# A graph layer and masked attention on one core: the row maximum is taken off the mask once, instead of off every score

## The chip, the core and the metric

The kernel runs on one core of a Trainium2 chip. Every time is in device microseconds (us) for one execution of the whole program; single instructions are given in nanoseconds (ns) where that reads better. A core has five engines with a queue each, worked off in order: TensorE (PE in the profile; PEld is its weight load) multiplies matrices into PSUM, VectorE (DVE) and ScalarE (ACT) read and write both PSUM and SBUF, GpSimd (POOL) works on SBUF only, and SyncE (SP) issues most of the DMAs. PSUM has eight banks of 128 partitions x 512 fp32 numbers. An engine waits for another through semaphores.

## What is computed

Two layers over 64 batch elements of 256 tokens with 512 features, all in fp32. The first mixes tokens with an adjacency matrix, the second is attention with 8 heads of 64 under a mask that is made of the same matrix. Cut to what matters here:

```python
h = jnp.maximum(_layernorm(x, axis=-1), 0.0)
x = x + einsum('bnd,do->bno', einsum('nm,bmd->bnd', adj, h), W0) + b0      # layer 0
h = jnp.maximum(_layernorm(x, axis=-1), 0.0)                               # layer 1
q = (h @ Wq + bq).reshape(b, n, H, HD)          # k and v in the same way
scores = einsum('bqhd,bkhd->bhqk', q, k) / sqrt(HD)
scores = scores + (1.0 - adj)[None, None, :, :] * -1000000000.0
attn = softmax(scores, axis=-1)
x = x + einsum('bhqk,bkhd->bqhd', attn, v).reshape(b, n, d) @ Wo + bo
```

The entries of `adj` are numbers between 0 and 1, not only 0 and 1. So the mask (1 - adj) * -1e9 differs by far more than any score between two entries of a row, and nearly all of a row's weight falls on its largest mask entry. A softmax may subtract any number from a row. The kernel doesn't subtract the maximum of the scores but the maximum of the mask's row, which it finds once.

## The kernel before

The 64 batch elements are taken in 32 groups of two (`NG = 32`, `GB = 2`). Layer 0 runs over all groups first (the loop `for g in range(NG - 1)`), then layer 1 over all groups.

**Order by hand.** The program text is the order of every engine's queue. The work that follows a matrix product (moments, exponentials, sums) is put later with `after(delay, ...)`, which queues a call for a later `tick()`. Pieces of work that belong to no group go into `side[g]`: the mask is prepared in seven steps at `side[20]` to `side[26]`, each issued on VectorE at the start of the turn of one group of layer 0. The products of layer 1 follow orders written out as strings (`QK` for queries and keys, `VO`, `V1`, `O1`, `OL` for values and outputs). A token such as `qGe` is one instruction: q is the product, G a block of it, e a step. `x` in these strings issues the next waiting exponential on ScalarE (`next_exponent`). 30 of the 32 groups get their queries and keys by `QK`, which holds this stretch:

```python
"... kGa x qCe qGc kCe qGd kCf kGi qCf kGj | qGe kGk kGb qFk kCg qp100 qGf kCh ..."
```

`qGe` is a copy of half the bank `q_Gs` by ScalarE (line 690), and `qGf` a matrix product (line 653) that adds into that half. It has to wait for the copy.

**Banks.** `bank()` hands out the PSUM banks in the order in which they were given back. With `seed=` it takes only a bank that was written as a whole last time, and ScalarE writes the seed into it (line 306); the first matmul then adds to what is there (`start=False`). `give()` puts a bank back when its last reader has been issued.

**Scores.** `score(g, qd)` is called 64 times (32 groups, `qd` for half of the heads). It makes four score blocks (c, b), each of two banks, with keys on the partitions and queries along the row. For blocks (0,0) and (0,1) ScalarE first fills four banks with the mask divided by the scale (`score_seeds`), TensorE adds the scores (line 1176), and VectorE's eviction multiplies by the scale and subtracts the row maximum `top` (line 1184). Blocks (1,0) and (1,1) get no seed: VectorE's eviction multiplies and adds the mask `maskT` (line 1187), and a further instruction subtracts `top` from the block of 128 x 1024: on GpSimd (line 1194) in 125 cases, on VectorE (line 1192) in three. The exponential in place follows on ScalarE (line 1210), the sum over two key halves on GpSimd (line 1217).

**Attention.** `attend(g, qd)` multiplies the exponentials with ones (`pden`, line 1226) and with the values (`pav`, line 1233). ScalarE copies the denominator (line 1240). Logarithm, exponential and a correction step on GpSimd invert it (`invert`, lines 1248 to 1252), and VectorE multiplies (line 1271). The next `score` follows `attend` directly on TensorE.

**Check.** Sums of denominators and reciprocals are kept in `stats`. At the end one comparison with `BOUND` over all of them decides whether the whole input is computed once more by `general_path`, with an ordinary softmax. With the inputs of the reference it isn't.

Of the kernel before, what the change touches and what calls it, by code (L numbers as in the profile page):

```python
# [8 lines left out]
F32 = mybir.dt.float32  # L9
I32 = mybir.dt.int32  # L10
AF = mybir.ActivationFunctionType
ALU = mybir.AluOpType
AX = mybir.AxisListType
P = 128
# [2 lines left out]
MASKED = -1000000000.0  # L17

BOUND = 1.0e15


def load_weight(nc, pool, w, name):
# [223 lines left out]
def kernel(  # L246
# [25 lines left out]
    HQ = 2  # L272
# [2 lines left out]

    nc.scalar.preload_act_table_set("natural_log_exp_and_others")
    keep = ctx.enter_context(tc.tile_pool(name="keep", bufs=1))
    stats = keep.tile([P, 2, NG * HQ], F32, name="stats")
    flag = keep.tile([1, 1], I32, name="flag")

    main = ExitStack()
# [14 lines left out]
    def bank(shape, name, seed=None, times=1.0, partial=False, full=False):  # L296

        if seed is not None or full:
            i = next(i for i in free_banks if whole[i])
        else:  # L300
            i = next((i for i in free_banks if not (partial and whole[i])), free_banks[0])
        free_banks.remove(i)
        t = psum.tile(shape, F32, tag=f"bank{i}", name=name)
        bank_of[id(t)] = (i, t)
        if seed is not None:
            nc.scalar.mul(t, seed, times)  # L306
        return t

    def give(t, all_written=True):
        i = bank_of.pop(id(t))[0]  # L310
        free_banks.append(i)
        whole[i] = all_written
# [5 lines left out]
    def after(delay, fn, *args):  # L318
        entered[0] += 1
        later.append((clock[0] + delay, entered[0], fn, args))  # L320
# [71 lines left out]

    maskT = const.tile([P, NT, N], F32, name="maskT")
    maskT_f = maskT.rearrange("p k n -> p (k n)")
    top = const.tile([P, N], F32, name="top")
    top_b = top[:, None, :].to_broadcast([P, 2 * NT, N])

    def masks():
        adj_sb = tmp.tile([P, NT, N], F32, tag="u", name="adj_sb")
        nc.sync.dma_start(adj_sb, adj.rearrange("(t p) m -> p t m", p=P))  # L400
        yield
        pm = bank([P, NT, N], "pm")
        for k in range(NT):
            for t in range(NT):
                nc.tensor.transpose(pm[:, k, t * P:(t + 1) * P], adj_sb[:, t, k * P:(k + 1) * P], ident)
        nc.vector.tensor_scalar(maskT, pm, -1.0, 1.0, op0=ALU.mult, op1=ALU.add)
        give(pm, False)
        yield
        nc.vector.tensor_scalar(maskT, maskT, MASKED, None, op0=ALU.mult)
        yield  # L410
        nc.vector.tensor_scalar(adj_sb, adj_sb, -1.0, 1.0, op0=ALU.mult, op1=ALU.add)
        yield
        nc.vector.tensor_scalar(adj_sb, adj_sb, MASKED, None, op0=ALU.mult)
        yield
        rowmax = small.tile([P, NT], F32, tag="rowmax", name="rowmax", bufs=1)
        nc.vector.tensor_reduce(rowmax, adj_sb, AX.X, ALU.max)
        spread = tmp.tile([P, NT, P], F32, tag="u", name="spread")
        nc.vector.tensor_copy(spread, rowmax[:, :, None].to_broadcast([P, NT, P]))
        yield
        pt = bank([P, N], "pt")  # L420
        for t in range(NT):
            nc.tensor.transpose(pt[:, t * P:(t + 1) * P], spread[:, t, :], ident)
        nc.vector.tensor_copy(top, pt)
        give(pt, False)


    L1 = {}
# [724 lines left out]

    A, AS, behind_seeds, behind_scores, exponents = {}, {}, [], [], []

    def score_bank(g, qd, c, b, **how):
        return [bank([P, NT * N], f"sc_{g}_{qd}_{c}{b}_{j}", **how) for j in range(2)]

    def score_seeds(g, qd, n=2):
        return {cb: score_bank(g, qd, *cb, seed=maskT_f, times=1.0 / SCALE) for cb in ((0, 0), (0, 1), (1, 0))[:n]}

    def score(g, qd, sums=(5, 6, 7, 8), exps=(3, 4, 5, 8), masked=None):


        pair = [act.tile([P, GB, 2 * NT, N], F32, tag="h", name=f"a_{g}_{qd}_{c}", bufs=2) for c in range(2)]

        masked = masked or score_seeds(g, qd)
        while behind_seeds:
            behind_seeds.pop(0)()
        for c in range(2):
            for b in range(GB):  # L1170
                seen = (c, b) in masked
                ps = masked[c, b] if seen else score_bank(g, qd, c, b)
                q, k = Q[g][qd, b], K[g][qd, b]
                for kt in range(NT):
                    for j in range(2):
                        nc.tensor.matmul(ps[j][:, kt * N:(kt + 1) * N],  # L1176
                                         k[j * HD:(j + 1) * HD, c, kt * P:(kt + 1) * P],
                                         q[j * HD:(j + 1) * HD, c, :], start=(kt == 0 and not seen), stop=True,
                                         skip_group_check=True)
                a = A[c, b] = pair[c][:, b]  # L1180
                for j in range(2):
                    o = a[:, j * NT:(j + 1) * NT, :]
                    if seen:
                        nc.vector.scalar_tensor_tensor(o, ps[j].rearrange("p (k n) -> p k n", k=NT), SCALE,  # L1184
                                                       top_b[:, 0:NT, :], op0=ALU.mult, op1=ALU.subtract)
                    else:
                        nc.vector.scalar_tensor_tensor(o.rearrange("p k n -> p (k n)"), ps[j], SCALE, maskT_f,  # L1187
                                                       op0=ALU.mult, op1=ALU.add)
                    give(ps[j])
                if not seen:  # L1190
                    if (g == NG - 1 or (g, qd) == (0, 0)) and b == 1:
                        after(0 if qd else 2, lambda a: nc.vector.tensor_tensor(a, a, top_b, op=ALU.subtract), a)
                    else:
                        nc.gpsimd.tensor_tensor(a, a, top_b, op=ALU.subtract)  # L1194
                if exps is None:
                    exponents.append((a, clock[0] + sums[2 * c + b], g, qd, c, b))
                else:
                    after(exps[2 * c + b], exponent, a)
                    after(sums[2 * c + b], key_sum, g, qd, c, b)
        while behind_scores:  # L1200
            behind_scores.pop(0)()
# [97 lines left out]
        side[4 + 4 * i].append((lambda n: weight_sums(nc.gpsimd, L1[n][0], n, [2 + STEPS * j for j in range(4)]), n))  # L1299
    for i in range(2):  # L1300
        side[13 + i].append((lambda: next(bias_steps, None),))
    for i in range(7):
        side[20 + i].append((lambda: next(mask_steps, None),))

    idle = bank([P, NT, N], "idle")
# [54 lines left out]
    first, second = queries_keys(0)  # L1360
    run(plain(0, *first))
    run(steps)
    second = plain(0, *second)
    run(second, 6)
    seeds = score_seeds(0, 0)
    run(second)
    score(0, 0, (4, 5, 6, 7), (3, 4, 5, 6), seeds)
    tick()
    hidden_sums(1, 6, 6, 7, 7)
    run(plain(0, *values(0)))  # L1370
# [1 line left out]
    for g in range(NG):  # L1372
# [2 lines left out]
        if g + 2 < NG:  # L1375
            load_hidden(g + 2)
        if g == NG - 1:
            score(g, 1, (2, 3, 5, 4), (1, 2, 4, 3), score_seeds(g, 1, 2))
        else:
            score(g, 1, exps=None if g + 1 >= FIRST2 else (3, 4, 5, 8))  # L1380
        tick()
# [26 lines left out]
            run(last)  # L1408
        attend(g, 1)
        if g + 1 < NG:  # L1410
            score(g + 1, 0, (5, 6, 7, 8) if g + 1 < NG - 1 else (1, 1, 1, 1), None if g + 1 >= FIRST2 else (3, 4, 5, 8),
                  score_seeds(g + 1, 0, 2) if g + 1 == NG - 1 else None)
            tick()

            def multiplied(g=g):
                del HH[g + 1]
                H2.pop(g + 1, None)
                if g + 2 < NG:
                    hidden_sums(g + 2, 1, 1, 1, 1)
                    if g + 2 >= FIRST2:  # L1420
                        block_hidden(g + 2, 2)

            n, halves, *rest = values(g + 1)
            if g + 1 < FIRST2:
                steps = plain(g + 1, n, halves, *rest)
                run(steps, 5)
                seeds = seed_outputs(g)
                run(steps)
                multiplied()
            else:  # L1430
                steps = quartered(g + 1, n, halves, H2[g + 1], *rest, multiplied=multiplied)
                if FIRST2 <= g < NG - 2:
                    steps.update(quartered_outputs(g))
                    run(follow(steps, VO))
                else:
                    steps = follow(steps, V1)
                    run(steps, 6)
                    if g < FIRST2:
                        seeds = seed_outputs(g)
                    run(steps)  # L1440
            if g < FIRST2:
                run(plain_outputs(g, seeds))
# [1 line left out]
    last = follow(quartered_outputs(NG - 1), OL)  # L1444
    run(last, 2)

    bad = small.tile([P, 2 * NG * HQ], F32, tag="bad", name="bad", bufs=1)
    worst = small.tile([P, 1], F32, tag="worst", name="worst", bufs=1)
    nc.vector.tensor_scalar(bad, stats.rearrange("p s i -> p (s i)"), BOUND, None, op0=ALU.is_le)
    nc.vector.tensor_reduce(worst, bad, AX.X, ALU.min)  # L1450
    nc.vector.tensor_scalar(worst, worst, -1.0, 1.0, op0=ALU.mult, op1=ALU.add)
    run(last, 3)
# [39 lines left out]
```

## Time and profile before

| what | value |
|---|---|
| median of three runs | 2607.23 us (2605.9 to 2607.35) |
| the profiled execution, device time | 2605.43 us |
| its span from first to last instruction | 2603.7 us |
| start of the first score (layer 1 under way) | 637.5 us |
| ScalarE seeds of score banks, line 306 | 256 x 591 ns |
| VectorE evictions, line 1184 with `top` / line 1187 with `maskT` | 256 x 684 ns / 256 x 681 ns |
| GpSimd subtractions of `top`, line 1194 | 125 x 2368 ns |
| VectorE subtractions of `top`, line 1192 | 3, of 1.22 to 2.30 us |
| exponentials waiting for line 1194 | 12.2 us in 37 waits, longest 0.7 |

A share of busy time says what an engine did, not what it held up: GpSimd is 80% busy, and most of this may lie beside TensorE's work. What counts for the time is where TensorE starts later than it could. Such a place can hide in a busy share, since the records of successive matmuls overlap: it shows as a longer mean of one group, or as a longer step from one start to the next.

### The profile page before, as it was taken

What the parts mean: (1) busy time and instruction counts of PE and PEld (TensorE: products, weight loads), DVE (VectorE), ACT (ScalarE), POOL (GpSimd) and SP (SyncE); (2) the same over time, 40 slices, a digit from 0 to 9 for tenths busy, and PEclk for the clock granted to TensorE, in tenths of its full rate; (3) what the DMA queues carried; (4) which work ended last, traced back from release to release, by engine and by line L of the source; (5) the groups of instructions that cost most, each with busy time, mean ns of one, the idle gap of its engine ahead of it and who ended that gap; (6) DMA issues with size and microseconds to landing.
All of it is one profiled execution on the core that took longest, in us unless ns stands there. A gap on an engine that the chain in (4) does not pass through costs nothing.

```text
span 2603.7 us, 57470 instructions
## 1 busy us (share of the span) xinstructions
PE 2586.1 (99%) x21914; PEld 2303.6 (88%) x21914; DVE 1908.9 (73%) x4154; ACT 1381.1 (53%) x3198; POOL 2082.9 (80%) x2275
## 2 busy tenths in 40 slices
PE   8999999999999999999999999999999999999998
PEld 7999899998888888888888888888888888888886
DVE  6888888885566777777776777777776777777777
ACT  4545454443455555555555555555555555555553
POOL 6788887774798888888877888888888888888776
PEclk9999999999999999999999999999999999999999
DMA  5776666565112222111111111111122222111101
GB/s 147 194 195 183 167 170 181 161 163 126 33 51 60 62 60 64 50 50 50 50 50 50 50 50 50 50 50 50 49 52 66 62 61 58 50 50 50 50 34 50
DMA packets 281112, 211.40 MB, mean 81 GB/s; under 512 B 145920, under 2 KB 212992, under 8 KB 280832
## 3 DMA queue, kind: packets, MB, share of 16 engines
q1 hardware_dynamic: 280224, 206.89, 30.0%
q8 instruction: 175, 2.87, 0.5%
q10 hardware_dynamic: 608, 0.79, 0.1%
q14 instruction: 105, 0.86, 0.1%
HBM read 106.96 MB, written 100.66 MB: 80 GB/s over the span
## 4 chain that ended last, share of the span: by engine, by line


## 5 line engine op out<-in xcount | busy, mean ns | idle before, releaser
L1184 DVE SCALAR_TENSOR_TENSOR a<-sc,top 128x512 f32<-128x512 f32 x256 | 159.0, 684 | 261.8 <-PE sc L1176 257.8
L1217 POOL TENSOR_TENSOR as<-a 128x512 f32<-128x512 f32 x256 | 319.5, 1280 | 6.3 <-ACT a L1210 6.2
L1194 POOL TENSOR_TENSOR a<-a,top 128x1024 f32<-128x1024 f32 x125 | 293.3, 2368 | 36.3 <-DVE a L1187 36.3
L1250 POOL TENSOR_TENSOR as<-as 128x512 f32<-128x512 f32 x64 | 80.5, 1258 | 267.3 <-ACT as L1249 263.8
L1210 ACT ACTIVATE a<-a 128x1024 f32<-128x1024 f32 x256 | 272.0, 1063 | 18.1 <-POOL a L1194 12.2
L1176 PE MATMUL sc<-q,k 64*128 64x256 f32 x2048 | 239.4, 383 | 0.0
L1176 PEld LDWEIGHTS sc<-q,k 64*128 64x128 f32 x2048 | 196.5, 187 | 43.5 <-issue 26.3
L1233 PE MATMUL pav<-a,v 128*32 128x256 f32 x4096 | 232.7, 379 | 0.0
L1233 PEld LDWEIGHTS pav<-a,v 128*32 128x32 f32 x4096 | 133.1, 110 | 87.9
L1240 ACT ACTIVATE as<-pden 128x512 f32<-128x512 f32 x64 | 38.4, 599 | 286.4 <-PE pden L1226 286.4
L42 DVE BATCH_NORM_STATS2 st<-x 128x6 f32<-128x512 f32 x256 | 173.2, 676 | 9.0 <-DMA x<-in_x_dram 6.8
L1187 DVE SCALAR_TENSOR_TENSOR a<-sc,maskT 128x512 f32<-128x512 f32 x256 | 158.4, 681 | 0.0
L1007 ACT ACTIVATE h<-x,nb,rs 128x512 f32<-128x512 f32 x128 | 97.2, 807 | 98.6 <-POOL nb L54 98.5
L306 ACT ACTIVATE sc<-maskT 128x512 f32<-128x512 f32 x256 | 137.4, 591 | 0.0
L878 ACT ACTIVATE h<-x,nb,rs 128x512 f32<-128x512 f32 x124 | 90.8, 803 | 52.1 <-POOL nb L54 46.6
L941 POOL TENSOR_TENSOR hs<-h 128x512 f32<-128x512 f32 x31 | 39.4, 1270 | 73.0 <-ACT h L878 73.0
L1013 DVE STREAM_TRANSPOSE r<-h 128x512 f32<-128x512 f32 x128 | 84.5, 691 | 8.9 <-ACT h L1007 3.6
L1097 ACT ACTIVATE q<-q_pa,bq_c 128x256 f32<-128x256 f32 (+1 forms) x150 | 61.8, 456 | 49.2 <-PE q_pa L653 36.9
L1271 DVE TENSOR_TENSOR oT<-pav,as 128x512 f32<-128x512 f32 x128 | 82.2, 683 | 7.7 <-POOL as L1252 7.5
L602 POOL TENSOR_TENSOR spare<-h1T,spare 128x128 f32<-128x128 f32 x180 | 82.1, 456 | 7.0
L826 DVE TENSOR_TENSOR x<-o_pa,x 128x512 f32<-128x512 f32 (+1 forms) x121 | 82.5, 682 | 6.0 <-PE o_pa L667 4.9
L503 POOL TENSOR_TENSOR t_y<-yT,t_y 128x512 f32<-128x512 f32 (+1 forms) x65 | 83.0, 1276 | 2.8 <-ACT yT L913 0.3
(1630 smaller groups left out, 8735.1 us busy)
## 6 DMA issues: line engine op xcount, KB each, us to landing
residual<-x SPq DMA_DIRECT2D x256, 128.0 KB, 2.7
hidden<-r SPq DMA_DIRECT2D x128, 256.0 KB, 4.5
h1T<-hidden SPq DMA_DIRECT2D x64, 512.0 KB, 7.5
x<-residual SPq DMA_DIRECT2D x32, 1024.0 KB, 8.1
x<-in_x_dram SPq DMA_DIRECT2D x254, 128.0 KB, 3.0
out_dram<-x SPq DMA_DIRECT2D x62, 512.0 KB, 4.1
w_sb<-in_L_gnn_weight_dram SPq DMA_DIRECT2D x1, 1024.0 KB, 9.9
wq_sb<-in_L_gnn_Wq_dram SPq DMA_DIRECT2D x1, 1024.0 KB, 8.4
```

The costliest lines, as they stand in the source:

```text
L42: nc.vector.bn_stats(st, src)
L306: nc.scalar.mul(t, seed, times)
L878: nc.scalar.activation(H0[g][:, t, :], xt[:, t, :], AF.Relu, bias=nb[:, t % n:t % n + 1], scale=rs[:, t % n:t % n + 1])
L1007: nc.scalar.activation(h1[:, k * NT + t, :], xt[:, k * NT + t, :], AF.Relu, bias=nb[:, t:t + 1], scale=rs[:, t:t + 1])
L1013: nc.vector.transpose(r[:, :, k, t, :], h1[:, k * NT + t, :].rearrange("p (j b) -> p j b", b=32))
L1176: nc.tensor.matmul(ps[j][:, kt * N:(kt + 1) * N], k[j * HD:(j + 1) * HD, c, kt * P:(kt + 1) * P], q[j * HD:(j + 1) * HD, c, :], start=(kt ...
L1184: nc.vector.scalar_tensor_tensor(o, ps[j].rearrange("p (k n) -> p k n", k=NT), SCALE, top_b[:, 0:NT, :], op0=ALU.mult, op1=ALU.subtract)
L1187: nc.vector.scalar_tensor_tensor(o.rearrange("p k n -> p (k n)"), ps[j], SCALE, maskT_f, op0=ALU.mult, op1=ALU.add)
L1194: nc.gpsimd.tensor_tensor(a, a, top_b, op=ALU.subtract)
L1210: nc.scalar.activation(a, a, AF.Exp)
L1217: nc.gpsimd.tensor_tensor(AS[c, b], a4[:, :, 0, :], a4[:, :, 1, :], op=ALU.add)
L1233: nc.tensor.matmul(po[f][h * 32:(h + 1) * 32, b * N:(b + 1) * N], v[:, k, h * HD + f * 32:h * HD + f * 32 + 32], A[h // 2, b][:, (h % 2) * ...
```

## The change

The row maximum is subtracted from the mask itself, once, when the mask is prepared: `maskT` then holds mask minus row maximum. All four score blocks are now evicted in the same way: scale, add `maskT`. The seeds on ScalarE, the tile `top` and the separate subtractions on GpSimd and VectorE are gone. With that a score block takes any two banks that are free, two at a time, and its first matmul overwrites.

The sums are not the same in rounding: before, the score was added to a mask entry of up to 1e9 in size, and lost its small digits, before the maximum was taken off. So two new steps of the preparation (now nine, at `side[20]` to `side[28]`) count in each row the mask entries within 1000 (`CLOSE`) of the maximum. A row with more than one, unless its maximum is 0, sets an entry of `ties` to 1e20. `ties` lies behind `stats` in one tile, `checks`, and the comparison with `BOUND` at the end covers both.

```diff
-    top = const.tile([P, N], F32, name="top")
-    top_b = top[:, None, :].to_broadcast([P, 2 * NT, N])
...
     def masks():
...
-        nc.vector.tensor_copy(top, pt)
+        for k in range(NT):
+            nc.vector.tensor_tensor(maskT[:, k, :], maskT[:, k, :], pt, op=ALU.subtract)
         give(pt, False)
+        yield
+        near = small.tile([P, NT], F32, tag="near", name="near", bufs=1)
+        nc.vector.tensor_scalar(near, rowmax, -CLOSE, None, op0=ALU.add)
+        for t in range(NT):
+            nc.vector.tensor_scalar(adj_sb[:, t, :], adj_sb[:, t, :], near[:, t:t + 1], None, op0=ALU.is_ge)
+        yield
+        nc.vector.tensor_reduce(near, adj_sb, AX.X, ALU.add)
+        nc.vector.tensor_scalar(near, near, -1.0, None, op0=ALU.add)
+        nc.vector.tensor_tensor(near, near, rowmax, op=ALU.mult)
+        nc.vector.tensor_tensor(near, near, near, op=ALU.mult)
+        nc.vector.tensor_scalar(ties, near, 1.0, 1.0e20, op0=ALU.min, op1=ALU.mult)
...
-    def score_bank(g, qd, c, b, **how):
-        return [bank([P, NT * N], f"sc_{g}_{qd}_{c}{b}_{j}", **how) for j in range(2)]
-
-    def score_seeds(g, qd, n=2):
-        return {cb: score_bank(g, qd, *cb, seed=maskT_f, times=1.0 / SCALE) for cb in ((0, 0), (0, 1), (1, 0))[:n]}
-
-    def score(g, qd, sums=(5, 6, 7, 8), exps=(3, 4, 5, 8), masked=None):
+    def score(g, qd, sums=(5, 6, 7, 8), exps=(3, 4, 5, 8)):
...
-                seen = (c, b) in masked
-                ps = masked[c, b] if seen else score_bank(g, qd, c, b)
+                ps = [bank([P, NT * N], f"sc_{g}_{qd}_{c}{b}_{j}") for j in range(2)]
...
-                                         q[j * HD:(j + 1) * HD, c, :], start=(kt == 0 and not seen), stop=True,
+                                         q[j * HD:(j + 1) * HD, c, :], start=(kt == 0), stop=True,
...
-                    if seen:
-                        nc.vector.scalar_tensor_tensor(o, ps[j].rearrange("p (k n) -> p k n", k=NT), SCALE,
-                                                       top_b[:, 0:NT, :], op0=ALU.mult, op1=ALU.subtract)
-                    else:
-                        nc.vector.scalar_tensor_tensor(o.rearrange("p k n -> p (k n)"), ps[j], SCALE, maskT_f,
-                                                       op0=ALU.mult, op1=ALU.add)
+                    nc.vector.scalar_tensor_tensor(o.rearrange("p k n -> p (k n)"), ps[j], SCALE, maskT_f,
+                                                   op0=ALU.mult, op1=ALU.add)
                     give(ps[j])
-                if not seen:
-                    if (g == NG - 1 or (g, qd) == (0, 0)) and b == 1:
-                        after(0 if qd else 2, lambda a: nc.vector.tensor_tensor(a, a, top_b, op=ALU.subtract), a)
-                    else:
-                        nc.gpsimd.tensor_tensor(a, a, top_b, op=ALU.subtract)
...
-    for i in range(7):
+    for i in range(9):
         side[20 + i].append((lambda: next(mask_steps, None),))
...
-    bad = small.tile([P, 2 * NG * HQ], F32, tag="bad", name="bad", bufs=1)
+    bad = small.tile([P, 2 * NG * HQ + NT], F32, tag="bad", name="bad", bufs=1)
...
-    nc.vector.tensor_scalar(bad, stats.rearrange("p s i -> p (s i)"), BOUND, None, op0=ALU.is_le)
+    nc.vector.tensor_scalar(bad, checks, BOUND, None, op0=ALU.is_le)
```

More of the change, by code (lines that the diff above doesn't have):

```diff
@@ L19 @@
 BOUND = 1.0e15
+CLOSE = 1000.0
 def load_weight(nc, pool, w, name):
@@ L277 @@
     keep = ctx.enter_context(tc.tile_pool(name="keep", bufs=1))
-    stats = keep.tile([P, 2, NG * HQ], F32, name="stats")
+    checks = keep.tile([P, 2 * NG * HQ + NT], F32, name="checks")
+    stats = checks[:, 0:2 * NG * HQ].rearrange("p (s i) -> p s i", s=2)
+    ties = checks[:, 2 * NG * HQ:]
     flag = keep.tile([1, 1], I32, name="flag")
@@ L1153 @@
     A, AS, behind_seeds, behind_scores, exponents = {}, {}, [], [], []
-    def score_bank(g, qd, c, b, **how):
-        return [bank([P, NT * N], f"sc_{g}_{qd}_{c}{b}_{j}", **how) for j in range(2)]
-    def score_seeds(g, qd, n=2):
-        return {cb: score_bank(g, qd, *cb, seed=maskT_f, times=1.0 / SCALE) for cb in ((0, 0), (0, 1), (1, 0))[:n]}
-    def score(g, qd, sums=(5, 6, 7, 8), exps=(3, 4, 5, 8), masked=None):
+    def score(g, qd, sums=(5, 6, 7, 8), exps=(3, 4, 5, 8)):
         pair = [act.tile([P, GB, 2 * NT, N], F32, tag="h", name=f"a_{g}_{qd}_{c}", bufs=2) for c in range(2)]
-        masked = masked or score_seeds(g, qd)
         while behind_seeds:
@@ L1362 @@
     run(steps)
[L1363 to L1367, printed above, removed]
+    run(plain(0, *second))
+    score(0, 0, (4, 5, 6, 7), (3, 4, 5, 6))
     tick()
@@ L1377 @@
         if g == NG - 1:
-            score(g, 1, (2, 3, 5, 4), (1, 2, 4, 3), score_seeds(g, 1, 2))
+            score(g, 1, (2, 3, 5, 4), (1, 2, 4, 3))
         else:
@@ L1410 @@
         if g + 1 < NG:
-            score(g + 1, 0, (5, 6, 7, 8) if g + 1 < NG - 1 else (1, 1, 1, 1), None if g + 1 >= FIRST2 else (3, 4, 5, 8),
-                  score_seeds(g + 1, 0, 2) if g + 1 == NG - 1 else None)
+            score(g + 1, 0, (5, 6, 7, 8) if g + 1 < NG - 1 else (1, 1, 1, 1), None if g + 1 >= FIRST2 else (3, 4, 5, 8))
             tick()
```

## The prediction, made before the changed kernel had run

> **What bounds the kernel now.** I read the page's shares first, then the form-by-form groups of TensorE, then stretches of the timeline where those groups differ.
>
> ```profile
> span 2603.7 us, 57470 instructions
> ...
> PE 2586.1 (99%) x21914; PEld 2303.6 (88%) x21914; DVE 1908.9 (73%) x4154; ACT 1381.1 (53%) x3198; POOL 2082.9 (80%) x2275
> ...
> PEclk9999999999999999999999999999999999999999
> ```
>
> TensorE is busy 99% of the span at full clock; only 17.6 us are idle, most of it in the first and the last 100 us. So nothing that GpSimd or ScalarE saves counts by itself: it counts where TensorE waits for it. A busy share hides short waits, because a matmul record that started late still overlaps its neighbours. The groups show them (line, engine, operation, names, shape, count, busy us, mean ns of one, idle before):
>
> ```profile
> L653 PE MATMUL q_Gs<-spare,spare 128*128 128x128 f32 x120 | 25.9, 298 | 0.0
> ...
> L653 PE MATMUL k_Gs<-spare,spare 128*128 128x128 f32 x120 | 23.2, 275 | 0.0
> ```
>
> These are the same multiplication for queries and for keys, and one is 23 ns longer on average: 120 x 23 ns = 2.8 us. The timeline of one group shows why (start, length, engine, line, what):
>
> ```profile
> 854.87 4.69 POOL L1194 TENSOR_TENSOR a<-a,top 128x1024 f32<-128x1024 f32 x2
> ...
> 859.59 1.06 ACT L1210 ACTIVATE a<-a 128x1024 f32<-128x1024 f32 x1 [0.37 <-POOL a L1194]
> ...
> 860.54 0.39 PE L653 MATMUL k_Cs<-spare,spare 128*128 128x128 f32 x2
> 860.56 0.25 ACT L690 COPY q_G<-q_Gs 128x128 f32<-128x128 f32 x1
> ...
> 860.86 0.49 PE L653 MATMUL q_Gs<-spare,spare 128*128 128x128 f32 x2
> ...
> 861.18 0.39 PE L653 MATMUL k_Gs<-spare,spare 128*128 128x128 f32 x2
> ```
>
> GpSimd's two subtractions of `top` end at 859.56. The exponential waits 0.37 us for the second, the copy of `q_Gs` stands behind the exponential on ScalarE, and TensorE may overwrite that bank only after the copy: 860.56 + 0.25 = 860.81, and it starts at 860.86. Two such matmuls normally start 0.22 us before what follows; here 0.32 pass before `q_Gs` and 0.32 within it (its pair reads 0.49 long, not 0.39): wait plus restart. From the records of single matmuls, 27 of the 30 runs of the order QK have this stall, 85 ns of wait on average and 101 ns of restart. The three without it are a test that the kernel made itself. In two, the exponential did not wait. The third is this:
>
> ```profile
> 2029.39 1.06 ACT L1210 ACTIVATE a<-a 128x1024 f32<-128x1024 f32 x1 [0.24 <-POOL a L1194]
> ...
> 2030.35 0.25 ACT L690 COPY q_G<-q_Gs 128x128 f32<-128x128 f32 x1
> ...
> 2030.95 0.39 PE L653 MATMUL q_Gs<-spare,spare 128*128 128x128 f32 x2
> ```
>
> The exponential started earlier against TensorE's place, and the pair is 0.39 again. Last, the end of the kernel, where VectorE takes one subtraction itself:
>
> ```profile
> 2566.14 1.75 DVE L1192 TENSOR_TENSOR a<-a,top 128x1024 f32<-128x1024 f32 x1
> ...
> 2567.98 1.06 ACT L1210 ACTIVATE a<-a 128x1024 f32<-128x1024 f32 x1 [1.49 <-DVE a L1192]
> ...
> 2568.94 0.25 ACT L690 COPY o_F<-o_Fs 128x128 f32<-128x128 f32 x1
> ...
> 2569.24 0.49 PE L653 MATMUL o_Fs<-spare 128*128 128x128 f32 x2 [0.44 <-ACT o_F L690]
> ```
>
> The same shape: subtraction, exponential, copy, TensorE.
>
> **What the Trainium skill says.** "Perfetto Trace Analysis", section Identifying the Most-Contended Engine, says that matmul busy time is a poor measure because pipelined matmuls look smaller than they are, and to take the share of weight loads; here that is 88%, which agrees that TensorE is the bound. Its section Optimization Strategy says to look for the gaps of that engine and the semaphore behind each, which is the way taken above. "SBUF — State Buffer", section SBUF: two separate sides, says that VectorE with two SBUF inputs and GpSimd lock each other out of a shared port pair for a whole instruction. The trace agrees: the three VectorE subtractions (L1192) took 1.22, 1.75 and 2.30 us for one shape.
>
> **The change part by part.**
>
> *Seeds.* 256 ScalarE writes into score banks (591 ns each, 137 us in the span) go. They stand between the denominator copy and the logarithm, while TensorE is in `pav`: at 1490.43 to 1492.58 for a score that starts at 1493.08. TensorE's step from the last `pav` matmul to the first score matmul is 309 ns in all 63 cases, and 309 ns also from `pav` to an output product, which follows no seeds. So it is the change of tiling, and nothing is gained there: 0.
>
> *Score evictions.* The 256 with `top` become ones with `maskT`: 684 against 681 ns, the same place, 0. TensorE's and SyncE's instruction orders are the same before and after.
>
> *Subtractions on GpSimd.* 125 x 2368 ns go. Wherever the exponential waited, it now depends on VectorE's eviction alone, which ended at 852.76 in the group above, long before. ScalarE's own previous work (L1097) ends at 859.23, so the exponential starts 0.37 earlier, the copy ends at 860.44, and TensorE wants the bank at about 860.76. The stall goes with 0.3 us to spare: 27 x (85 + 101) ns = -5.0 us. Next late would be the same copy, 0.3 us away, or the block sums on GpSimd, which also come earlier.
>
> *Subtractions on VectorE (3).* In the last group's value phase, 1.22 us at 2547.13 delays two VectorE adds, and TensorE waits there for `v_Cs` twice, 195 + 101 and 222 + 101 ns. With it gone a ScalarE copy of `v_pc` is next late; the same place in an earlier group (762.47) shows 111 + 101 ns for it. Net -0.4. In the last score (fences above) the stall of 601 + 101 ns goes: the exponential can start behind the copy at 2566.22, about 2566.5. -0.7. The later VectorE stalls of that stage (0.32, 0.35 and 0.37 us) come from a queue that is full from 2570.17 on, behind an add that waits for TensorE and ScalarE, so I leave them. The third, at 643.7, made TensorE wait nowhere.
>
> *Mask preparation.* On VectorE in layer 0 a 0.39 us copy becomes two subtractions from a bank (about 0.4 each by a like add, L826 128x256 at 0.41). Two new steps follow one and two groups later: a tiny add with two comparisons of 128x256, then a reduction (0.65, as L416) and four tiny ones (0.15 each, as L1451). By halving L413 (0.80) and L409 (1.45) a comparison takes 0.4 to 0.7, so the steps cost about 1.0 to 1.6 and 1.3 us of VectorE. Behind them waits the add of `w_g_a`, which TensorE needs before it adds into that bank. Before, that add ended at 529.7 and 548.4 for matmuls at about 531.4 and 550.05: 1.6 us to spare, already waiting for GpSimd's sums of `y`. Lower end 0. Upper end: both steps overrun by about a microsecond through the shared port, 2 us with restarts. The dearest old mask step cost TensorE at most 0.33 (493.71). I take +0.7.
>
> *The flags.* 130 instead of 128 columns in one 0.23 us instruction: 0. SBUF: `top` goes, two columns come: 0.
>
> Sum: -5.0 - 0.4 - 0.7 + 0.7 = -5.4 us. The profiled execution took 2605.43 us (span 2603.7 and 1.7 around it), which would become 2600.0. It stands 1.8 us under the median of the three runs, so for a median of runs I add that back: **2601.8 us**.
>
> **The rivals.**
> - *The wait is replaced, nothing is won.* If another release reached TensorE within the next tenth of a microsecond, the 5.0 us would shrink to some 1, and mask steps would take that back: 2607. Against it: all 27 stalls follow ScalarE's copy by 52 to 53 ns, and the three without the late copy have none.
> - *More is won.* If the last stage's VectorE stalls (1.0 us), both `v_pc` stalls (0.4) and the cost in layer 0 (0.7) vanish as well: 2599.7, to 2598.5 if the `o_pa` stall at 2563.84 (0.45 + 0.10) goes too and the mean wait is a little longer than counted. For it: GpSimd holds the shared port 293 us less. Against it: those stalls stand behind full queues.
> - *Slower: a new wait for a bank.* Seeds claimed whole banks, four together. Now the second pair of every score takes other banks, those of `k_Es`, `q_Es` or `o_Es`, `o_pb`, and TensorE waits directly for VectorE's last reads. If these came late, each of the 59 scores whose banks change would pay a wait and 0.1 of restart. At 0.19 each this is 11.2, net +5.8: 2613.0; slower than before from 0.09 each on. Against it: those reads end at 1490.3 or 1520.6, the second pair starts near 1494.0 and 1524.9, so they would have to slip by over 3.7 us.
> - *The fast path is left.* If a row had two near maxima, the general path would compute all again, far over twice the time. The inputs of the reference exclude it: the closest two entries of a row differ by 112,356 in mask units, the limit is 1000.
>
> **How the numbers follow.** The forecast 0.68, more won 0.15, nothing won 0.12, a bank or the general path 0.05. About 0.2% (5.2 us, so below 2602.0) is what a measurement here can tell from no change. The forecast lies at its edge: its size varies by some 1.5 us through layer 0 and run to run, so I give 0.43 of its 0.68 to faster and 0.25 to same. Faster 0.43 + 0.15 = 0.58, same 0.25 + 0.12 = 0.37, slower 0.05. The range runs from 2598.5 (more won) to 2606.5 (half of the case of nothing won).
>
> **What would show it.** Right: `q_Gs` from `spare` at 275 ns like `k_Gs`; no exponential waiting for GpSimd or for a VectorE subtraction; GpSimd near 1790 us busy and ScalarE near 1244, while TensorE's order stays; groups of the middle 0.19 us shorter, about 61.4 instead of 61.57 us (922.41 to 983.98); `o_Fs` in the last score's stage without its 0.44. Wrong: `q_Gs` still at 298; first score matmuls later than 309 ns after `pav`, or gaps inside a score; layer 0 ending over 1 us later than at 637.5.

## The result, and the profile after

| | before | after |
|---|---|---|
| median, measured together | 2607.23 us (2604.88 to 2608.52) | 2599.46 us (2598.81 to 2599.94) |
| ratio | | 0.9971, 95% interval 0.9960 to 0.9981 |
| profiled execution, span | 2603.7 us | 2597.0 us |
| GpSimd / ScalarE busy | 2082.9 / 1381.1 us | 1792.4 / 1254.3 us |

The changed kernel is faster by 7.8 us between these medians. In a second comparison (2599.01 us beside a before of 2605.43) it was 6.4 us, ratio 0.9975 (0.9965 to 0.9984). Between the two profiled executions it is 6.6.

The page of the changed kernel: span, busy shares, and the groups of the evictions and exponentials (busy us, mean ns | idle before, and what ended it). Line numbers differ a little from those of before.

```profile
span 2597.0 us, 56864 instructions
...
PE 2580.3 (99%) x21914; PEld 2299.8 (89%) x21914; DVE 1903.8 (73%) x4160; ACT 1254.3 (48%) x2942; POOL 1792.4 (69%) x2150
...
L1188 DVE SCALAR_TENSOR_TENSOR a<-sc,maskT 128x512 f32<-128x512 f32 x512 | 311.9, 681 | 259.9 <-PE sc L1181 255.7
...
L1206 ACT ACTIVATE a<-a 128x1024 f32<-128x1024 f32 x256 | 272.6, 1065 | 3.6 <-DVE a L1188 3.6
```

GpSimd is lighter by 290 us and ScalarE by 127 (137 were forecast; each row of four seeds had overlapped its neighbours' records by some 0.17 us). TensorE's share stays at 99%, and so the whole change has to be looked for in short waits. All 512 evictions now have one form, and the exponentials wait for it alone. The form-by-form groups of TensorE, the same two as before:

```profile
L666 PE MATMUL q_Gs<-spare,spare 128*128 128x128 f32 x120 | 23.2, 275 | 0.0
...
L666 PE MATMUL k_Gs<-spare,spare 128*128 128x128 f32 x120 | 23.2, 275 | 0.0
```

The 23 ns are gone. The timeline of the same stretch shows how (start, length, engine, line, what):

```profile
859.29 1.08 ACT L1206 ACTIVATE a<-a 128x1024 f32<-128x1024 f32 x1
...
860.32 0.27 ACT L703 COPY q_G<-q_Gs 128x128 f32<-128x128 f32 x1
...
861.01 0.39 PE L666 MATMUL k_Cs<-spare,spare 128*128 128x128 f32 x2
...
861.23 0.39 PE L666 MATMUL q_Gs<-spare,spare 128*128 128x128 f32 x2
```

The exponential waits for nothing. The copy ends at 860.59, and TensorE comes at 861.23, 0.22 us after the pair ahead of it. The pair itself reads 0.39 again.

In layer 0 the two new steps of the mask can be seen. VectorE and GpSimd at the first of them, then at the second:

```profile
528.47 1.27 POOL L516 TENSOR_TENSOR t_y<-yT 128x512 f32<-128x512 f32 x1
...
528.79 0.97 DVE L429 TENSOR_SCALAR near<-rowmax 128x2 f32<-128x2 f32 x1
...
529.80 1.70 DVE L431 TENSOR_SCALAR adj_sb<-adj_sb,near 128x256 f32<-128x256 f32 x2
...
529.82 1.27 POOL L516 TENSOR_TENSOR t_y<-yT,t_y 128x512 f32<-128x512 f32 x1
...
531.42 0.68 DVE L839 TENSOR_TENSOR x<-w_27a,x 128x512 f32<-128x512 f32 x1
...
548.67 1.26 POOL L516 TENSOR_TENSOR t_y<-yT,t_y 128x512 f32<-128x512 f32 x1
...
549.24 0.72 DVE L434 TENSOR_SCALAR near<-near 128x2 f32<-128x2 f32 x1
...
550.00 0.16 DVE L435 TENSOR_TENSOR near<-near,rowmax 128x2 f32<-128x2 f32 x1
```

An addition over two columns takes 0.97 us. It ends at 529.76, and GpSimd's sum that runs beside it ends at 529.74; the one at 549.24 ends at 549.96, GpSimd's at 549.93. The 1.70 us of the two comparisons are uneven as well: the first took 1.44 us and ended at 531.24, just after GpSimd's next sum (531.09), the second took 0.35. So `x` gets its add of `w_27a` only at 531.42, and TensorE waits. From the list of its waits (what waited, for what: us in total, times, longest):

```profile
PE w_27a L523 <- DVE x L839: 1.2, 1, 1.2
```

The sum over all steps from one TensorE start to the next, after minus before, by stage (each from the records of single matmuls):

| stage | us |
|---|---|
| layer 0, first 60 us | -0.88 |
| rest of layer 0 | +1.42 |
| layer 1: `q_Gs` stalls | -5.03 |
| layer 1: inside the scores | -0.67 |
| layer 1, other | -0.05 |
| last group: `v_Cs` and `o_Fs` stalls, other | -1.14 |
| after the last matmul | -0.28 |
| span | -6.63 |

### The profile page after: what moved, and what is told of

The parts are those of the page before. It is cut to its first block, busy times and chain, and to the rows that moved or that the text cites. A ratio compares the mean times of both kernels' runs of the same rounds, so it can differ in the third digit from the quotient of the medians.

```text
span 2597.0 us, 56864 instructions
## 1 busy us (share of the span) xinstructions
PE 2580.3 (99%) x21914; PEld 2299.8 (89%) x21914; DVE 1903.8 (73%) x4160; ACT 1254.3 (48%) x2942; POOL 1792.4 (69%) x2150
## 4 chain that ended last, share of the span: by engine, by line
## 5 line engine op out<-in xcount | busy, mean ns | idle before, releaser
L1188 DVE SCALAR_TENSOR_TENSOR a<-sc,maskT 128x512 f32<-128x512 f32 x512 | 311.9, 681 | 259.9 <-PE sc L1181 255.7
L1246 POOL TENSOR_TENSOR as<-as 128x512 f32<-128x512 f32 x64 | 80.8, 1263 | 411.0 <-ACT as L1245 404.9
L516 POOL TENSOR_TENSOR oT<-oT 128x512 f32<-128x512 f32 x31 | 39.4, 1271 | 149.4 <-DVE oT L1267 149.4
L703 ACT COPY q_F<-q_Fs 128x128 f32<-128x128 f32 (+1 forms) x90 | 27.1, 301 | 157.6 <-PE q_Fs L666 157.6
L1248 POOL TENSOR_TENSOR as<-as 128x512 f32<-128x512 f32 x64 | 80.8, 1262 | 5.3
L516 POOL TENSOR_TENSOR t_h<-h1T,t_h 128x512 f32<-128x512 f32 x64 | 81.9, 1280 | 2.5
```

Source lines behind the costliest of these rows:

```text
L516: eng.tensor_tensor(self.t[n][:, c, :], self.operand(p, c), self.operand(q, c), op=ALU.subtract)
```

## The experiments

Each was timed beside the kernel before on its own chip: at 2605.07 us for the first three and the first move of the exponential, at 2607.16 for the later sum in the kernel before and the last move, at 2605.43 for the others. So times are compared as ratios, and stages by the traces: from here on, a gain or loss in a stage is a sum of TensorE's steps between starts, as in the table.

**The subtractions put back alone.** GpSimd subtracts a tile of zeros where it subtracted `top` before, 125 times, which costs its time and changes no number. The seeds stay out.

```diff
+    zero = const.tile([P, N], F32, name="zero")
+    nc.vector.memset(zero, 0.0)
+    zero_b = zero[:, None, :].to_broadcast([P, 2 * NT, N])
...
+                if c == 1 and not (b == 1 and (g == NG - 1 or (g, qd) == (0, 0))):
+                    nc.gpsimd.tensor_tensor(a, a, zero_b, op=ALU.subtract)
```

> The changed kernel with 125 GpSimd subtractions put back on blocks (1,0) and (1,1), of a tile of zeros, so that only their time comes back; no seeds. Theory A (the exponential waited because GpSimd came to the subtractions late, and the seeds on ScalarE delayed GpSimd too, through the inversion that stands behind them): GpSimd's inversion now ends 1.8 us earlier than in the kernel before (851.2 against 853.0 in the group at 850), so the second subtraction ends near 857.8 instead of 859.56 and the exponential at 859.3 waits for nothing: q_Gs from spare stays at 275 ns and the time within 1 us of the changed kernel (about 2599 to 2601). Rival B (the subtractions alone made the stall, as the prediction had it): q_Gs back near 298 ns, 5.0 us more, about 2604.5. Rival C (GpSimd's share of the SBUF port slows VectorE everywhere): 2 us or more without a stall at q_Gs.

Measured: 2603.01 us (2602.34 to 2604.54), ratio 0.9993 (0.9985 to 1.0001). The group of TensorE, and the timeline of the stretch:

```profile
L669 PE MATMUL q_Gs<-spare,spare 128*128 128x128 f32 x120 | 26.0, 299 | 0.0
```

```profile
849.92 1.27 POOL L1251 TENSOR_TENSOR as<-as 128x512 f32<-128x512 f32 x1
...
855.10 4.69 POOL L1195 TENSOR_TENSOR a<-a,zero 128x1024 f32<-128x1024 f32 x2
...
859.82 1.06 ACT L1211 ACTIVATE a<-a 128x1024 f32<-128x1024 f32 x1 [0.37 <-POOL a L1195]
...
861.09 0.49 PE L669 MATMUL q_Gs<-spare,spare 128*128 128x128 f32 x2
```

The stall is back in full: +2.15 us of wait and +2.84 of restart against the changed kernel, 4.99 in sum, again in 27 of the 30 runs. Outside `q_Gs`, layer 1 is no longer than in the changed kernel (0.28 us shorter), so GpSimd's work doesn't slow it there anywhere else. My own theory for this run fell. I had thought that without the seeds ScalarE would hand the denominators over earlier, and GpSimd would be done in time. But GpSimd starts the inversion at 849.92, right behind its own block sums (line 618, to 849.96). It was itself the late one, and an earlier ScalarE doesn't move it.

**The seeds put back alone.** ScalarE fills the four banks of blocks (0,0) and (0,1), and their eviction subtracts the zeros. The scores are the same sums in another order, with a subtraction of zeros that changes nothing.

```diff
+        masked = {(0, b): [bank([P, NT * N], f"sc_{g}_{qd}_0{b}_{j}", seed=maskT_f, times=1.0 / SCALE)
+                           for j in range(2)] for b in range(GB)}
...
+                                         q[j * HD:(j + 1) * HD, c, :], start=(kt == 0 and not seen), stop=True,
...
+                        nc.vector.scalar_tensor_tensor(o, ps[j].rearrange("p (k n) -> p k n", k=NT), SCALE,
+                                                       zero_b[:, 0:NT, :], op0=ALU.mult, op1=ALU.subtract)
```

> The changed kernel with ScalarE's 256 seeds put back for blocks (0,0) and (0,1); they hold the new mask over the scale, and the eviction of these blocks subtracts a tile of zeros, as the old one subtracted the row maximum. No subtractions on GpSimd. Theory A (no exponential waits for GpSimd, so its lateness through the seeds hurts nobody): within 1 us of the changed kernel, at most 0.7 more inside the scores; q_Gs at 275 ns. Rival (the seeds cost TensorE time themselves, at the start of a score or through the banks): 64 scores x 0.05 to 0.1 us, 3 to 6 us more, with the step from the last pav matmul to the first score matmul over 309 ns.

Measured: 2601.51 us (2599.34 to 2602.48), ratio 0.9985 (0.9979 to 0.9992), span 2599.4. The groups of `q_Gs` stay at 275 ns. Of the 2.4 us that its span is longer than the changed kernel's, 2.2 lie at one place, the very first score, whose seeds here stand directly ahead of it (in the kernel before they were issued earlier):

```profile
PE sc L1187 <- ACT sc L309: 1.4, 1, 1.4
```

My theory A hadn't foreseen that place. Inside the other scores it was right with its 0.7. The matmuls of the scores, in the changed kernel and in this one:

```profile
L1181 PE MATMUL sc<-q,k 64*128 64x256 f32 x2048 | 238.7, 383 | 0.0
...
L1187 PE MATMUL sc<-q,k 64*128 64x256 f32 x2048 | 239.7, 383 | 1.4 <-ACT sc L309 1.4
```

Without seeds a score takes 3348 ns from the start of its first matmul to that of its last (the middle value of 64); with them it takes 3359, as in the kernel before. That is 11 ns in each, about 0.7 in all. In the sum over the other 63 scores only 0.35 of it is to be seen, because the changed kernel lost 0.33 us in a single score, as the kernel before did in the score that starts at 2016 us, and this run did not; why, no run shows. So 127 us of ScalarE's time were worth some 0.7 us.

**The mask steps later in the turn.** In the changed kernel the two new steps are issued five ticks after the start of the turn.

```diff
-        side[20 + i].append((lambda: next(mask_steps, None),))
+        side[20 + i].append((lambda: next(mask_steps, None),) if i < 7 else (after, 5, next, mask_steps, None))
```

> The changed kernel with its two new mask steps issued five ticks later in their groups, where VectorE idles some 1.9 us behind the add of w_g_a. Theory A (the steps cost TensorE 1.43 and 0.72 us because the add of w_g_a stands behind them): both stalls in layer 0 go, but the common stall of about 0.33 us per group may come back in up to four groups: 0.8 to 2.1 us less than the changed kernel, about 2597.4 to 2598.7. Rival (they cost through the port or through GpSimd, wherever they stand): less than 0.5 us difference.

Measured: 2597.5 us (2597.16 to 2598.37), ratio 0.9971 (0.9960 to 0.9982), span 2596.6, only 0.4 shorter. Its timeline, with the first new step and the matmul that had waited for it:

```profile
531.40 1.59 PEld L523 LDWEIGHTS w_27a<-w_s,t_y 128*128 128x128 f32 x8 [0.27 <-POOL t_y L516]
...
541.14 0.15 DVE L429 TENSOR_SCALAR near<-rowmax 128x2 f32<-128x2 f32 x1
...
541.32 0.62 DVE L431 TENSOR_SCALAR adj_sb<-adj_sb,near 128x256 f32<-128x256 f32 x2
```

With GpSimd idle beside it (its next instruction starts at 542.26) the addition takes 0.15 us instead of 0.97, and the two comparisons 0.62 instead of 1.70. TensorE's steps at the two places are 1.11 and 0.40 us shorter than in the changed kernel. But its weight load now waits 0.27 us for GpSimd's sum `t_y`, as in many groups of layer 0 before. In the changed kernel the delay at the mask steps had let GpSimd get ahead, and the two groups that follow lacked that stall. Here it is back (+0.34 and +0.35 us). Behind the first 60 us, layer 0 is 0.14 us longer than before's, instead of 1.42 in the changed kernel; in this execution most of the difference was lost in those first 60 us (0.8). So theory A is shown in the trace alone: by the ratio this run can't be told from the changed kernel (0.9971 and 0.9975 in its two comparisons).

**That common stall itself.** One GpSimd sum of layer 0, `last_feature_sum`, is issued one tick later in the changed kernel, behind the two sums `t_y`.

```diff
-            after(5 if g else 7, last_feature_sum, g + 2)
+            after(6 if g else 7, last_feature_sum, g + 2)
```

> The changed kernel with GpSimd's last feature sum of a group (hs4) issued one tick later, behind the two sums t1 and t2 of y that TensorE waits for in layer 0. In the changed kernel TensorE has that wait of 0.14 to 0.34 us and 0.10 of restart in about 13 groups. If GpSimd's queue order makes it: these stalls go, 3 to 5 us less than the changed kernel, w_a<-w_s,t_y without long steps except at the two mask steps. If it is GpSimd's amount of work or VectorE's adds: the stalls stay, less than 1 us.

Measured: 2593.97 us (2593.92 to 2595.04), ratio 0.9958 (0.9945 to 0.9972), span 2592.2. It is the fastest here, 5.0 us under the changed kernel in the same comparison. All of the 4.86 us in the traces but 0.08 lie in layer 0. GpSimd in the changed kernel (first; the two sums `t_y` that follow, at 528.47 and 529.82, are shown above) and in this one:

```profile
527.24 1.27 POOL L957 TENSOR_TENSOR hs<-h,hs 128x512 f32<-128x512 f32 x1
```

```profile
522.59 1.26 POOL L954 TENSOR_TENSOR hs<-hs,h 128x512 f32<-128x512 f32 x1
...
523.82 1.26 POOL L516 TENSOR_TENSOR t_y<-yT 128x512 f32<-128x512 f32 x1
...
525.17 1.27 POOL L516 TENSOR_TENSOR t_y<-yT,t_y 128x512 f32<-128x512 f32 x1
...
528.23 1.27 POOL L957 TENSOR_TENSOR hs<-h,hs 128x512 f32<-128x512 f32 x1
```

The sum `hs` (line 957) stood ahead of `t_y`, for which TensorE waits; now it stands behind. The wait at `w_27a` went as well (1.35 us), and 0.39 us of the one a group later.

**Both edits together**, the two diffs above.

> The changed kernel with both: the two new mask steps five ticks later and GpSimd's last feature sum one tick later. If the two stalls at the mask steps (1.43 and 0.72 us) and the common one (about 0.35 us per group) are separate, both gains add: 5 to 6.5 us less than the changed kernel, since the common stall cannot come back where a mask step had hidden it. If not, about the better of the two alone.

Measured: 2594.44 us (2593.69 to 2595.29), ratio 0.9958 (0.9945 to 0.9972): no better than the later sum alone, which was the second of the two cases expected. The later sum had already taken most of the wait at the mask steps. Both edits together win another 0.4 us there, and lose as much to new waits at `w_29c` and `w_30c`. So the two gains are for the most part one.

**The later sum in the kernel before.**

> The kernel before, with the last feature sum of layer 0 one tick later, the edit that brought the changed kernel to 2594. Theory (the two gains are independent: one lies in layer 0, one in layer 1): layer 0 about 4.5 us shorter, 2600.7 us. Rival (the gain in the changed kernel came from taking away the cost of its new mask steps together with the stalls around them): 2602.5 or more.

Measured: 2603.53 us (2601.9 to 2604.62), ratio 0.9986 (0.9979 to 0.9993), a gain of 3.6 us beside its own before, where theory had 4.7 and rival 2.9 or less: between the two. After the first 60 us its layer 0 is 3.06 us shorter than before's. The changed kernel with this edit is 3.50 shorter than before's there, and 4.9 shorter than the changed kernel's first trace (4.3 than its second). So some 3 us of the gain have nothing to do with the change, and the rest is mostly the cost of its own mask steps. In the profiled execution 1.3 us are lost again in layer 1: the waits ahead of `q_Gs`, 85 ns on average before, are 133 here. GpSimd's subtractions stand some 0.05 us later there against TensorE's place; why, I did not find out.

**The exponential moved by a few instructions.** In the kernel before, one `x` of `QK` goes behind `qGe`. Then it can't hold up the copy of `q_Gs`.

```diff
-    "qFl kCc kp101 kCd kGa x qCe qGc kCe qGd kCf kGi qCf kGj | qGe kGk kGb qFk kCg qp100 qGf kCh kGc qp101 qCg "
+    "qFl kCc kp101 kCd kGa qCe qGc kCe qGd kCf kGi qCf kGj | qGe x kGk kGb qFk kCg qp100 qGf kCh kGc qp101 qCg "
```

> The kernel before, untouched but for one token of the order QK: the fourth exponential x stands behind the copy qGe instead of ahead of qCe. All seeds and subtractions stay. Theory A (TensorE lost its time only to that copy standing behind a waiting exponential): the 27 stalls of 186 ns go, 5.0 us less, about 2602.2; q_Gs at 275 ns, while the exponential may still wait for GpSimd. Rival (the relief of GpSimd and ScalarE itself shortens the kernel): no change, about 2607.

Measured: 2611.69 us (2610.75 to 2613.07), ratio 1.0026 (1.0016 to 1.0035). The groups:

```profile
L653 PE MATMUL k_Gs<-spare,spare 128*128 128x128 f32 x120 | 26.2, 301 | 3.8
...
L653 PE MATMUL q_Gs<-spare,spare 128*128 128x128 f32 x120 | 23.2, 275 | 0.0
```

Neither expectation came: the kernel is 6.6 us slower. The stall of `q_Gs` is gone, all 5.03 us of it, and a dearer one has come for `k_Gs`, whose copy now stands behind the same exponential: 8.7 us of wait and 3.0 of restart. So it is the exponential's place on ScalarE that decides which copy is late, and the next place only moves the wait.

**The exponential moved further**, behind `qBe`, where no copy is wanted soon.

```diff
-    "qFl kCc kp101 kCd kGa x qCe qGc kCe qGd kCf kGi qCf kGj | qGe kGk kGb qFk kCg qp100 qGf kCh kGc qp101 qCg "
+    "qFl kCc kp101 kCd kGa qCe qGc kCe qGd kCf kGi qCf kGj | qGe kGk kGb qFk kCg qp100 qGf kCh kGc qp101 qCg "
...
-    "kBf qDe qBd | qDf kBg kCi kCj qBn kCk qBe kBh kCl kBi qDg qBf | qDh qEa qBg kEa kBj qEb kDa kEb kBk qBh qBi "
+    "kBf qDe qBd | qDf kBg kCi kCj qBn kCk qBe x kBh kCl kBi qDg qBf | qDh qEa qBg kEa kBj qEb kDa kEb kBk qBh qBi "
```

> The kernel before but for one token: the fourth exponential x of QK stands behind qBe, where ScalarE idles about 1.1 us in the trace of before, and not behind qGe, where its 1.06 us held up the next copy (k_Gs, +8.7 + 3.0 us in the run with the token near). Seeds and subtractions stay. Theory A (TensorE lost time only to a copy that stood behind the waiting exponential): q_Gs and k_Gs both at 275 ns, about 5.0 us less than the kernel before in layer 1, from the place of one instruction. Rival (the exponential's place only passes the wait on to another copy, so that GpSimd's work has to go): the steps of layer 1 sum to no gain, or to a loss.

Measured: 2601.67 us (2600.56 to 2602.9), ratio 0.9986 (0.9980 to 0.9993). `q_Gs` and `k_Gs` both read 275 ns. After the first turn of `QK`, the kernel gains 0.19 us in each group, 5.11 us in all by the last, as theory A had it. But the first turn itself loses 1.76, which no expectation had. Its timeline:

```profile
749.94 0.45 POOL L327 TENSOR_TENSOR spare<-wv_s,spare 128x128 f32<-128x128 f32 x1
...
750.35 1.26 POOL L1217 TENSOR_TENSOR as<-a 128x512 f32<-128x512 f32 x1
...
751.67 0.41 PE L1226 MATMUL pden<-as,ones 128*32 128x256 f32 x2 [1.15 <-POOL as L1217]
```

In that turn GpSimd makes sums of the value weights' blocks (line 327), which it does once only. The key sum (line 1217), whose exponential now comes later, stands behind them, and TensorE waits for it at `pden`.

**The same, but not in the first turn.**

```diff
-            run(follow(steps, QK))
+            run(follow(steps, QK if g == 1 else QK_FAR))
```

`QK_FAR` (its lines are left out here) is the order of the run before.

> The kernel before, with the fourth exponential of QK moved behind qBe in every turn of QK but the first (g = 1). In the run with the move in all turns the groups from the second on became 0.19 us shorter each, but the first turn lost 1.76 us, where GpSimd was still making block sums of the value weights and the key sum that TensorE wants came too late. Theory (the exponential's place alone made the stall, and the subtractions on GpSimd were harmless except as its cause): no wait at pden in that turn, q_Gs from spare at about 276 ns, 2600.3 us in the median where before stands at 2605.4, as much as the changed kernel's layer 1 gains. Rival (a tighter key sum costs in other turns too once the first no longer shifts them): 2601.5 or more, with pden waits elsewhere.

Measured: 2600.87 us (2600.18 to 2601.95) beside 2607.16, ratio 0.9975 (0.9966 to 0.9985). The wait at `pden` is gone, `q_Gs` from `spare` reads 275 ns, and layer 1 is 4.98 us shorter, all of it in the steps to and within `q_Gs`. That is the gain that the changed kernel has at this place, yet all seeds and all subtractions are still in it. In layer 1 as a whole the changed kernel gains 6.9 us: 0.7 more in the scores and 1.1 more in the last group. The ratio is that of the changed kernel's second comparison, but ratios here can't tell 2 us apart. I had written 2600.3 where before stands at 2605.4, a gain of 5.1; it is 6.3 by medians and 4.3 in the spans of the traces.

**The changed kernel again**, as the one to compare the last runs with.

> The changed kernel once more as it is, to compare on one chip in one set of runs: 0.996 to 0.998 of the kernel before; TensorE's steps in layer 1 as in its first trace within 0.2 us.

Measured: 2599.01 us (2598.09 to 2599.61), as told above. Layer 1 agrees with the first trace to 0.02 us; the first 60 us of layer 0 differ by 0.53, and the rest of layer 0 is 0.80 longer than before's instead of 1.42.

## Why the prediction was right

**The stall of `q_Gs`.** Forecast -5.0, measured -5.03 (wait 2.29, restart 2.74). The chain subtraction, exponential, copy, TensorE is shown from both sides. The subtractions alone bring it back (4.99), and moving the exponential alone takes it away while the subtractions stay. It is the one large term, and 290 us less on GpSimd are worth just this. The groups of the middle are 61.36 us apart, as named. The margin was larger than the 0.3 us of the forecast: the copy now ends 0.65 us before TensorE's start, and with a stall it was 0.05.

**Seeds, evictions, flags: 0.** Right at the start of a score: the fixed 309 ns from `pav` to the first score matmul did stay, with no seeds before it. What the prediction missed is inside the score. The last three pairs of matmuls in the last block start 7 ns apart instead of 17 or 18; for two of them the next step makes up for it, for the last it doesn't, and a score is 11 ns shorter, 0.67 us in the table's sum. This belongs to the seeds, and the forecast's 0 for them was short by that much: with the seeds back the pairs are 17 apart again and a score has its 3359 ns; with the subtractions back they stay at 7. The block itself has no seed in any of these kernels. By which way the seeds reach it (the writes, the order of the banks or the other eviction came back together), no run shows.

**The three subtractions on VectorE.** Forecast -0.4 in the last group's value phase. There the two stalls (195 + 101 and 222 + 101 ns) went and a new one of 110 + 101 came at `v_Bs`, the place that was named: -0.41. Forecast -0.7 at `o_Fs`; -0.70 came. Three lines of the changed kernel's timeline there answer the fence of before:

```profile
2560.73 1.06 ACT L1206 ACTIVATE a<-a 128x1024 f32<-128x1024 f32 x1
...
2562.32 0.27 ACT L703 COPY o_F<-o_Fs 128x128 f32<-128x128 f32 x1 [0.53 <-PE o_Fs L666]
...
2562.99 0.38 PE L666 MATMUL o_Fs<-spare 128*128 128x128 f32 x2
```

The exponential that had waited 1.49 us for VectorE starts at once, and the copy behind it ends 0.40 us before the pair, which reads 0.38 and carries no wait. The stalls behind it that were to stay (0.32, 0.35 and 0.37 us) stayed.

**The mask steps.** Forecast +0.7 with an upper end of 2. The place and the way were right: the add of `w_27a`, and the same add a group later. The steps were dearer than I took them, +1.1 and +0.4 us where 0.7 stood for both. Of the comparisons, for which I had 0.4 to 0.7 us each, one took 1.44 beside GpSimd's sum and the other 0.35: work was forecast a little too high, and the wait for GpSimd, which stood only in the upper end, came. A common stall of layer 0 then fell out twice and gave 0.7 back. Net, the rest of layer 0 cost 1.42 in one trace and 0.80 in another of the same kernel (0.85 and 0.86 with the subtractions or the seeds back, the very first score left out): near the forecast, but in part by luck, through an offset that I hadn't seen.

**The rivals.** "Nothing is won" failed on all 30 runs of `QK` at once, since nothing was late next. A new wait for a bank did not come; the list of TensorE's waits in the changed kernel has none at `sc`, and the steps inside the scores became shorter, not longer. "More is won" was right in its number, 2599.7, but not by its reasons: of the stalls it named, only those already in the forecast went.

**The size.** The forecast was 2.3 us too high. Its sum for one execution was -5.4, and the traces differ by -6.6: 0.67 inside the scores, 0.28 after the last matmul and 0.88 in the first 60 us, less the dearer mask steps (0.7). The first 60 us, where TensorE waits for its first inputs, differ from before's by -1.4 to +0.2 us between the traces of these kernels, and by 0.53 between two traces of the changed kernel alone; that part of the gain I count as scatter. The rest lies in adding back 1.8 us for before's median: the changed kernel's profiled execution was only 0.6 under its own. Beside a before of 2605.43 the gain was 6.4, so the 7.8 of the first comparison contains such scatter too.

## What to carry to other kernels

Before removing work from an engine that isn't the bound, find the instruction of the bound engine that waits for it: here 417 us of busy time were taken off two engines, and 5.0 of the some 6.6 us that came of it were to be had by moving one exponential in a list. A stall of a tenth of a microsecond that recurs in every group doesn't show as idle time; compare the mean of two groups that do the same multiplication, and mend it by moving what stands ahead of the late copy, then look at what is late next. A one-time preparation that shares an engine with the moved work (the value weights' sums) can take back a third of the gain in a single turn.

## What the runs showed of the hardware

A VectorE addition over 2 columns, SBUF to SBUF, took 0.97 us beside a running GpSimd sum, 0.67 in the run with the later sum and 0.15 with GpSimd idle. Both slow ones ended within 0.03 us of GpSimd's instruction, and so did the one of 0.72 us shown above. A comparison over 256 columns took 1.44 us, ending 0.15 after GpSimd's sum, and 0.35 without a sum beside it. The Trainium skill ("SBUF — State Buffer", section SBUF: two separate sides) says that VectorE and GpSimd share a pair of ports, which VectorE takes in a mode that uses two ports or with two SBUF inputs, and that the pair is an exclusive lock held for the whole instruction. The times agree with such a lock. The addition has one tensor as input, so by this it would have to be in the two-port mode; no trace shows the mode. So here the time of a tiny instruction was set by what ran beside it and not by its own work.

A wait of TensorE costs more than its length. The pair of matmuls behind it is stretched by 102 ns after a wait of 110 ns (`v_Bs`) and by 104 after one of 828 (`o_pa`, near the end), and by some 75 in a few places (after the wait of the mask step at `w_27a`, for one). In the 27 stalls of `q_Gs` the restart (2.74 us) was more than the wait (2.29).
